# A weave planner's TensorE prices and three buffers are changed in a four-layer convolution kernel

## The chip, the cores and the metric

The kernel runs as one program on one core of a Trainium2 chip. A core has five engines that work side by side, each through its own instructions in the order in which they were written: TensorE (matrix products, PE in the profile, with its weight loads as PEld), VectorE (DVE), ScalarE (ACT), GpSimd (POOL) and SyncE (SP), which here only issues DMA transfers. An engine waits for another by a semaphore. The metric is the device time of one execution in microseconds; three executions of the kernel before took 6713.72, 6719.5 and 6728.77, a median of 6719.5.

## The reference

The input x has 16 images of 32 channels of 128 x 128. Four layers follow one another, each of the form x = x + layer(groupnorm(x)):

```python
x = x + _L0_conv_ref(_gn(x), W2, b2, W1, b1)        # a recurrence over 128 skewed columns
x = x + _L1_conv_ref(_gn(x), weight)                # -sum |patch - w|, quantised, 3 x 3, 32 -> 32
x = x + _L2_conv_ref(_gn(x), weights1)              # Hartley transform, 32 x 32 modes mixed, back
x = x + _L3_conv_ref(_gn(x), conv1_w, ..., deconv3_b)  # edge filters, then a small U-shaped net
```

Layer 1 is the bulk: for each of 32 outputs, 32 inputs, 9 taps and every pixel, an absolute difference is added up. Layer 3 makes five filtered and normalised copies of its input, and then conv1 (160 to 32 channels, 3 x 3), three poolings and small convolutions (conv2 to conv4), three doublings of size, each followed by a convolution (conv5 to conv7), and multiplies the result with its input.

## The kernel before, in words

Channels lie on the 128 partitions, four images at a time: four groups of four images. The time falls into three parts.

**Layer 0** (function `stage0`) is a recurrence that needs everything else to wait. The change does not touch it.

**Layer 1 with later layers woven in.** Class `Differences` makes, for each half image (32 of them, two to an image, which the code calls a batch), 72 *maps*: relu(q - w) of 128 x 8192 numbers, made either by DVE (L760) or by ACT (L757). TensorE adds each map to four accumulators with 16 matmuls (`sums`, L647), and adds a linear term in 9 steps (`linear`, L662). A map lies in one of three tiles for DVE and two for ACT, so its maker can't go on when TensorE is more than that behind. Layers 2 and 3 of a group (class `After`) need all four images of that group from layer 1, and nothing else; so group 0's are put between the maps of group 1, and so on. What is not placed when the last map is made is left to the tail.

**The tail** (`drain`) writes out what is left of group 2's layers 2 and 3, and all of group 3's, taking a step of one and a step of the other by a planned time.

What decides the order is a planner that runs while the program is written, class `Weave`. It keeps planned clocks for TensorE, DVE and ACT. `After.work` is a generator: each of its parts issues instructions and then yields. A positive number is the planned TensorE time of what was issued; a negative one is a wait in planned time; SUMMED waits until the planned sums are done; ("done", v) until a put-off piece is done; ("after", n) until batch n is finished. After each map, `Weave.advance` is given the time at which TensorE is next needed for a map's sum, and places steps as long as they fit:

```python
start = max(self.pe, self.ready)
if start + 1.0 > due + SLACK:
    return
us = self.step()
```

A map's sum costs PE_US of planned TensorE time (L708), a linear step what L669 says, and what is then left of the interval is filled by `keep_busy` (L671), up to four times four matmuls with a weight of zeros, which add nothing to the result and keep TensorE running. Pieces for DVE, ACT and SP are put off with `weave.later(us, ...)` and written when the planned time has come. The engines know nothing of the plan: `keep_order` fixes the order on each engine, and semaphores do the rest. So a plan that is wrong makes an engine wait, and never makes a wrong result.

The later layers of one group, with the lines at which they yield, are in order: `forward` (a transform of rows and columns, L1119, L1134, L1091), `mixing` (32 steps of 16 matmuls, L1206, whose weights of 1 MB a piece lie in a pool of "t_w" tiles), `back` (L1270, then L1315 with the residual from HBM), `statistics` (products of rows of the normalised image, L1420, to learn the five filters' means and deviations), the folding of those into conv1's weights (L1553, tables v loaded by POOL), the sums for the cut edges (L1713), `conv1` (8 chunks of 16 rows, each 25 taps of 16 matmuls, L1739, with its edges at L1756, pooled at L1666), conv2 to conv4 (`small_layers`, L1589), and the doublings with their convolutions (`round`, L905), the last of them in `last`, which multiplies with the input and stores (L1868, L1838).

`frames` holds a ring of tiles of 20 padded rows each, which `back` fills first, `statistics` normalises and refills (by `load` for chunks not seen, then by `again` for the first chunks of conv1), and `conv1` reads. How many tiles each pool has while the weave runs is in `buffers` (L966); in the tail group 3 has a larger set of its own (L513), which stays. GpSimd issues its table loads (L1408, L1492, L1538) [...]; all other DMAs but a few at the start are SP's.

## Time and profile before

| | us |
|---|---|
| median of three runs | 6719.5 |
| profiled execution | 6728.15 |
| its span, first to last instruction | 6726.4 |
| TensorE busy (its matmuls) | 5379.0 |
| DVE busy | 5537.9 |
| ACT busy | 5464.8 |
| POOL busy | 63.0 |
| first map starts | 685.0 |
| last map starts, on ACT | 5595.0 |
| mean granted TensorE clock | 0.919 |

Busy times are unions of an engine's instructions; a matmul's end is modelled, and matmuls in different parts of the array overlap, so a busy TensorE is not one at its peak. Lines such as L647 are lines of the kernel before. "A <- B" in a row of the profile is "written from", in a list of waits "waited for". The 40 slices of the page are 168 us each. Times in a window count from the first instruction.

### The profile page before, as it was taken

What the parts mean: (1) busy time and instruction counts of PE and PEld (TensorE: products, weight loads), DVE (VectorE), ACT (ScalarE), POOL (GpSimd) and SP (SyncE); (2) the same over time, 40 slices, a digit from 0 to 9 for tenths busy, and PEclk for the clock granted to TensorE, in tenths of its full rate; (3) what the DMA queues carried; (4) which work ended last, traced back from release to release, by engine and by line L of the source; (5) the groups of instructions that cost most, each with busy time, mean ns of one, the idle gap of its engine ahead of it and who ended that gap; (6) DMA issues with size and microseconds to landing.
All of it is one profiled execution on the core that took longest, in us unless ns stands there. A gap on an engine that the chain in (4) does not pass through costs nothing.

```text
span 6726.4 us, 271378 instructions
## 1 busy us (share of the span) xinstructions
PE 5379.0 (80%) x127212; PEld 2798.3 (42%) x127212; DVE 5537.9 (82%) x6839; ACT 5464.8 (81%) x3210; POOL 63.0 (1%) x67
## 2 busy tenths in 40 slices
PE   3798777788777879997877878998787785886896
PEld 3675333333343433333333433333334442453574
DVE  7898999999999889998999989999899995144122
ACT  3998999999999989999999999999899993121112
POOL 0000000000000000000000000000000000000000
PEclk9999899999989989998999889999899897997897
DMA  7553312212253632213453552221354353355314
GB/s 318 204 190 123 81 49 64 61 31 66 71 140 113 178 94 60 62 38 72 101 147 93 174 149 68 66 63 42 87 128 138 103 155 119 125 188 141 83 39 107
DMA packets 380776, 728.20 MB, mean 108 GB/s; under 512 B 73284, under 2 KB 225348, under 8 KB 368772
## 3 DMA queue, kind: packets, MB, share of 16 engines
q1 hardware_dynamic: 372180, 676.41, 35.2%
q0 software_dynamic: 7040, 33.80, 1.5%
q8 instruction: 995, 16.30, 1.0%
q14 instruction: 129, 1.06, 0.1%
q10 hardware_dynamic: 432, 0.64, 0.0%
HBM read 510.69 MB, written 200.00 MB: 106 GB/s over the span
## 4 chain that ended last, share of the span: by engine, by line
issue 33%; PE 29%; DVE 20%; ACT 14%; DMA 3%; SPq 1%; POOL 0%; DVEq 0%; ACTq 0%; POOLq 0%
DVE d_dve L760 12%; PE acc L1739 11%; ACT d_act L757 9%; PE acc L647 8%; PE acc L905 3%; PE pg L223 3%; ACT gt L237 2%; DMA v<-fold_d 1%; PE acc L1589 1%; PE acc L1420 1%; ACT junk L198 1%; DVE y L1677 1%; DVE stat L124 1%; DMA x_in<-in_x_dram 1%; ACT th L247 1%
## 5 line engine op out<-in xcount | busy, mean ns | idle before, releaser
L757 ACT ACTIVATE d_act<-q,neg 128x8192 f16<-128x8192 f16 (+1 forms) x629 | 4450.5, 7154 | 102.7 <-PE acc L647 81.1
L760 DVE TENSOR_SCALAR d_dve<-q,qw 128x8192 f16<-128x8192 f16 (+1 forms) x1675 | 3864.3, 2360 | 214.5 <-PE acc L647 195.6
L647 PE MATMUL acc<-d_dve,sel 128*32 128x512 f16 x26800 | 1879.4, 404 | 436.3 <-DVE d_dve L760 344.6
L647 PEld LDWEIGHTS <-sel 128*32 128x32 f16 x36864 | 1021.0, 101 | 2124.4 <-issue 1475.8
L1739 PE MATMUL acc<-xp,wf 32*32 32x512 f32 x25600 | 1001.7, 611 | 32.6 <-issue 27.2
L647 PE MATMUL acc<-d_act,sel 128*32 128x512 f16 x10064 | 740.0, 416 | 345.2 <-ACT d_act L757 333.4
L1680 ACT ACTIVATE y<-pooled,b 32x128 f32<-32x128 f32 x472 | 188.7, 400 | 552.6 <-DVE pooled L1666 546.3
L1739 PEld LDWEIGHTS acc<-xp,wf 32*32 32x32 f32 x25600 | 417.6, 104 | 377.6 <-issue 295.8
L677 PE MATMUL acc<-q,zero 128*32 128x512 f16 x6720 | 484.2, 400 | 0.0
L905 PE MATMUL acc<-y,u_conv 32*32 32x256 f32 (+1 forms) x9728 | 358.7, 461 | 85.1 <-issue 68.7
L223 PE MATMUL pg<-h,wb 64*64 64x20 f32 (+15 forms) x8192 | 342.0, 306 | 58.0 <-DVE h L251 32.9
L237 ACT ACTIVATE gt<-pg,bias 128x20 f32<-128x20 f32 (+15 forms) x1024 | 332.7, 385 | 39.3 <-PE pg L223 37.1
L223 PEld LDWEIGHTS pg<-h,wb 64*64 64x64 f32 x8192 | 252.1, 151 | 133.5 <-DVE h L251 80.9
L677 PEld LDWEIGHTS <-zero 128*32 128x32 f16 x6720 | 200.6, 101 | 187.3 <-issue 42.7
L1868 DVE SCALAR_TENSOR_TENSOR xr<-acc,l_one,xr 128x512 f32<-128x512 f32 x128 | 87.2, 744 | 229.8 <-PE acc L905 179.7
L1420 PE MATMUL acc<-xp 32*64 32x204 f32 (+3 forms) x8576 | 240.8, 339 | 40.6 <-issue 40.5
L905 PEld LDWEIGHTS acc<-y,u_conv 32*32 32x32 f32 x9728 | 162.0, 109 | 216.9 <-issue 168.1
L1420 PEld LDWEIGHTS acc<-xp 32*64 32x64 f32 (+1 forms) x8576 | 169.1, 132 | 124.4 <-issue 118.9
L1838 ACT ACTIVATE xr<-xr,l_ms 128x1024 f32<-128x1024 f32 x64 | 68.7, 1146 | 182.1 <-DVE xr L1868 171.9
L223 PE MATMUL pg<-xn,wb 64*64 64x2 f32 (+63 forms) x4096 | 183.5, 290 | 25.6 <-issue 17.0
L1774 DVE TENSOR_TENSOR acc<-acc,cut 128x4 f32<-128x4 f32 x256 | 35.2, 164 | 200.6 <-PE acc L1739 198.3
L1589 PE MATMUL acc<-y,w_conv 32*32 32x512 f32 (+2 forms) x4608 | 153.6, 487 | 37.1 <-issue 28.9
(218 smaller groups left out, 3624.5 us busy)
## 6 DMA issues: line engine op xcount, KB each, us to landing
q<-q_d SPq DMA_DIRECT2D x128, 536.2 KB, 10.3
xp<-xn_d SPq DMA_DIRECT2D x64, 660.0 KB, 5.1
xp<-x_d SPq DMA_DIRECT2D x56, 640.0 KB, 5.3
xr<-xn_d SPq DMA_DIRECT2D x64, 528.0 KB, 11.3
x_in<-in_x_dram SPq DMA_DIRECT2D x16, 2048.0 KB, 14.7
xn<-in_xs_dram SPq DMA_DIRECT2D x64, 512.0 KB, 7.1
res<-in_x_dram SPq DMA_DIRECT2D x64, 512.0 KB, 8.6
x_d<-res SPq DMA_DIRECT2D x64, 512.0 KB, 4.8
```

The source lines that it names most:

```text
L223: nc.tensor.matmul(bank[c][q][64 * pair : 64 * pair + 64, :, :width], wb[half, 4 * kind + KIND[q]].rearrange("p b o -> p (b o)"), v[half], ...
L237: nc.scalar.activation(gt[:, q, :, :n], bank[c][q][:, :, :n], AF.Tanh if q == G else AF.Sigmoid, bias=bias[:, KIND[q] : KIND[q] + 1],)
L647: self.nc.tensor.matmul(acc[k][32 * j : 32 * j + 32, :], self.sel16[:, i // 9, :], d[:, row : row + 4, c : c + W], start=first, stop=last,)
L677: self.nc.tensor.matmul(acc[k][32 * j : 32 * j + 32, :], self.zero, q[:, :4, :W], start=False, stop=False)
L757: nc.scalar.activation(dst, src, AF.Relu, bias=self.neg[:, i : i + 1])
L760: nc.vector.tensor_scalar(dst, src, self.qw[:, i : i + 1], 0.0, ALU.subtract, ALU.max)
L905: nc.tensor.matmul(acc[blk][32 * j : 32 * j + 32, o : o + rows * n], t[part, 4 * par + tap, :], src[part, top : top + rows, left : left + ...
L1420: nc.tensor.matmul(gram[blk][j : j + width, at : at + n], xp[part, l, 2 + j : 2 + j + width], xp[part, rows, j : j + width + 4], start=sta ...
L1589: nc.tensor.matmul(acc[blk][32 * j : 32 * j + 32, : rows * n], wc[name][part, tap, :], src[part, at : at + rows, kw : kw + n], start=tap == 0,
L1680: nc.scalar.activation(d, s, AF.Identity, bias=bj)
L1739: nc.tensor.matmul(acc[blk][32 * j : 32 * j + 32, :], tap_of("all", tap)[rows], xp[rows, 4 * j + kh : 4 * j + kh + 4, kw : kw + W], start= ...
L1868: nc.vector.scalar_tensor_tensor(v, acc[blk].rearrange("p (b r w) -> p r w b", b=2, w=64), one[:, blk : blk + 1], v, ALU.add, ALU.mult,)
```

## The change

It has three parts. The first sets new planned TensorE times for most steps; no instruction's work changes by it, only where in the order the planner puts it, and how many matmuls by zeros it adds. A map's sum goes from 1.0 to 0.88, a linear step from 0.45 to 0.36, four matmuls by zeros from 0.25 to 0.22; among the later layers a mixing step goes from 1.0 to 0.3 (with five written waits that go from 2.5 to 5.5), a step of `back` from 1.1 to 0.35 and from 0.8 to 0.4, a row of `statistics` from 0.5 to 0.38, the cut sums from 0.6 to 0.35, a tap of conv1 from 1.15 to 1.06 and its edges from 0.3 to 0.1, and the convolutions after it get a new formula, which for 512 columns gives 1.06 in place of 1.15 and for 256 columns 0.67 in place of 0.65 (conv3) or 1.05 (`round`). The second gives the pool of mixing weights a fourth tile and the ring of frames a third while the weave runs. As 8 chunks are no multiple of 3 tiles, conv1 counts on where `statistics` stopped, with `window`, which takes chunk ch from the tile of chunk ch + 8. The third sets the memory for GpSimd's descriptors to 4,096 bytes of each partition, where it had the default.

```diff
--- before.py
+++ after.py
@@ -484,7 +484,7 @@
 
 
 
-DVE_US, ACT_US, PE_US = 2.36, 7.15, 1.0
+DVE_US, ACT_US, PE_US = 2.36, 7.15, 0.88
 LATE = 1.5
 SLACK, CLOCK = 3.0, 1.0
 SUMMED = ("summed",)
@@ -666,18 +666,18 @@
                     start=False,
                     stop=False,
                 )
-        self.weave.pe = max(self.weave.pe, self.weave.now) + 0.45
+        self.weave.pe = max(self.weave.pe, self.weave.now) + 0.36
 
     def keep_busy(self, acc, q, until):
 
 
         start = max(self.weave.pe, self.weave.now)
-        for k in range(min(int((until - start - 0.1) / 0.25), 4)):
+        for k in range(min(int((until - start - 0.1) / 0.22), 4)):
             for j in range(4):
                 self.nc.tensor.matmul(
                     acc[k][32 * j : 32 * j + 32, :], self.zero, q[:, :4, :W], start=False, stop=False
                 )
-            self.weave.pe = start + 0.25 * (k + 1)
+            self.weave.pe = start + 0.22 * (k + 1)
 
     def run(self, tc, ctx, weave):
         nc, R, P = self.nc, self.R, self.P
@@ -910,7 +910,7 @@
                         stop=tap == 3,
                         skip_group_check=True,
                     )
-            yield rows * n / 512 * 0.2 + 0.95
+            yield rows * n / 512 * 0.78 + 0.28
             if tap != 2:
                 continue
             for j in range(4):
@@ -963,7 +963,7 @@
         self.nc, self.tc, self.side, self.ps, self.cst, self.bias = nc, tc, side, ps, cst, bias
         self.a, self.d, self.stat, self.out = a, d, stat, out
         self.spare, self.banks = None, 0
-        self.buffers = {"t_x": 4, "xm": 3, "xw": 2, "t_w": 3, "t_r": 4, "frames": 2, "gm": 3, "e_v": 3, "l_x": 2}
+        self.buffers = {"t_x": 4, "xm": 3, "xw": 2, "t_w": 4, "t_r": 4, "frames": 3, "gm": 3, "e_v": 3, "l_x": 2}
         store = [d["up"][i] for i in range(3)]
         self.up5 = Composed(nc, sm, a, "deconv1", "conv5", bias[:, 7:8], bias[:, 4:5], store[0])
         self.up6 = Composed(nc, sm, a, "deconv2", "conv6", bias[:, 8:9], bias[:, 5:6], store[1])
@@ -1106,7 +1106,7 @@
                         steps[n] = weave.later(2.0, store)
 
                     steps[n] = outs[n] = weave.summed(out)
-                    return 1.45
+                    return 1.2
 
                 yield -4.0
                 t1s, ta, ready = {}, {}, {}
@@ -1124,7 +1124,7 @@
                         weave.dve += 0.7
 
                     ready[n, 0] = weave.summed(out)
-                    return 1.05
+                    return 0.9
 
                 def turned(n):
 
@@ -1133,7 +1133,7 @@
                     for a in range(4):
                         nc.tensor.transpose(p[:, 128 * a : 128 * a + 128], ta[n][:, a, :], cst["ident128"])
                     ready[n, 1] = weave.summed(lambda: scaled(n, p))
-                    return 1.5
+                    return 1.0
 
                 for n in range(10):
                     if n < 8:
@@ -1212,9 +1212,9 @@
                 )
             if ky % 4 == 3 and len(wt) < M1 // 4:
                 wt.append(self.weights(wp, len(wt)))
-            yield 1.0
+            yield 0.3
             if ky % 4 == 3 and 8 < ky < M1 - 1 and not weave.draining:
-                yield -2.5
+                yield -5.5
         yield SUMMED
         zs = wp.tile([128, 2, 4, 4, 32], F32, name="zs", bufs=1)
         for half in range(2):
@@ -1274,7 +1274,7 @@
                                 start=True,
                                 stop=True,
                             )
-                    yield 1.1
+                    yield 0.35
                 yield SUMMED
                 for blk in range(4):
                     dst = o1[:, :, blk, 16 * oh : 16 * oh + 16].rearrange("p h o -> p o h")
@@ -1319,7 +1319,7 @@
                             start=True,
                             stop=True,
                         )
-                yield 0.8
+                yield 0.4
                 if previous:
                     yield -3.2
                     take_out(*previous)
@@ -1347,6 +1347,7 @@
             nc.vector.memset(t[:, :, W + 3], 0.0)
 
         chunk = lambda ch: ring[ch % len(ring)]
+        window = lambda ch: ring[(ch + 8) % len(ring)]
 
         def parts(ch, half):
 
@@ -1386,9 +1387,9 @@
         def again(ch, half):
 
             own = slice(10 * half, 10 * half + 10)
-            nc.sync.dma_start(chunk(ch)[:, own, :], padded(ch, own.start, own.stop))
-
-        return load, normalise, store, again, chunk
+            nc.sync.dma_start(window(ch)[:, own, :], padded(ch, own.start, own.stop))
+
+        return load, normalise, store, again, chunk, window
 
     def statistics(self, g, pool, frames, sides, out, tables):
 
@@ -1399,7 +1400,7 @@
 
 
         nc, cst, weave = self.nc, self.cst, self.weave
-        load, normalise, store, again, chunk = frames
+        load, normalise, store, again, chunk, _ = frames
         ahead = self.buffers["frames"]
         ready = {(n // 2, n % 2): normalise(n // 2, n % 2, 0.5 + 4.0 * n) for n in range(2 * ahead)}
         tables_ahead = self.buffers["gm"]
@@ -1441,7 +1442,7 @@
                 first, last = len(own), min(H - r, 3)
                 if first < last:
                     products(xp, l, slice(l + first, l + last), 64, 68 * first, False, r == H - 3)
-                yield 0.5
+                yield 0.38
                 if l not in (9, 17):
                     continue
 
@@ -1593,7 +1594,7 @@
                                 start=tap == 0,
                                 stop=tap == 8,
                             )
-                    yield rows * n / 512 * 1.0 + 0.15
+                    yield rows * n / 512 * 0.78 + 0.28
                 yield SUMMED
                 for blk in range(4):
                     evict(r, rows, acc[blk][:, : rows * n], blk)
@@ -1690,7 +1691,7 @@
             size = PARTS[n][4] * PARTS[n][5]
             return wf[:, const if i == size else at + i, :]
 
-        _, _, _, again, chunk = frames
+        _, _, _, again, _, window = frames
         ahead = self.buffers["frames"]
         p = self.acc()
         for j in range(4):
@@ -1718,7 +1719,7 @@
                             stop=tap == 10,
                             skip_group_check=True,
                         )
-                yield 0.6
+                yield 0.35
         yield SUMMED
         cut = pool.tile([128, 4, 2, 8, 4], F32, name="cut")
         for blk in range(4):
@@ -1727,7 +1728,7 @@
 
         spreads = []
         for ch in range(H // R):
-            xp = chunk(ch)
+            xp = window(ch)
 
             acc = [self.acc() for _ in range(4)]
             edge = {0: ("t", 0, 0, 1), H // R - 1: ("b", 3, 3 * W, 17)}.get(ch)
@@ -1761,8 +1762,8 @@
                                     stop=False,
                                     skip_group_check=True,
                                 )
-                            yield 0.3
-                yield 1.15
+                            yield 0.1
+                yield 1.06
             yield SUMMED
             if ch + ahead < H // R:
                 for half in range(2):
@@ -2031,7 +2032,7 @@
     from concourse.bass_utils import run_bass_kernel_spmd
 
     arrays, at = layout(inputs)
-    nc = bacc.Bacc("TRN2", target_bir_lowering=False, num_devices=1)
+    nc = bacc.Bacc("TRN2", target_bir_lowering=False, num_devices=1, dynamic_dma_scratch_size=4096)
     arrays = {f"in_{n}_dram": t for n, t in arrays.items()}
     a = {}
     for n, t in arrays.items():
```

## The prediction

> **What bounds the kernel now.** I read the 40 slices first, then the costliest groups, then busy time by stretch, then the waits of the long stretch, and last the order of time on TensorE.

> ```profile
> PE   3798777788777879997877878998787785886896
> DVE  7898999999999889998999989999899995144122
> ACT  3998999999999989999999999999899993121112
> PEclk9999899999989989998999889999899897997897
> ```

> Three parts show: a recurrence (slices 1 to 4), a long part in which DVE and ACT are full (to slice 33), and a tail in which they are nearly idle and only TensorE works.

> ```profile
> L757 ACT ACTIVATE d_act<-q,neg 128x8192 f16<-128x8192 f16 (+1 forms) x629 | 4450.5, 7154 | 102.7 <-PE acc L647 81.1
> L760 DVE TENSOR_SCALAR d_dve<-q,qw 128x8192 f16<-128x8192 f16 (+1 forms) x1675 | 3864.3, 2360 | 214.5 <-PE acc L647 195.6
> ```

> These are the 2,304 difference maps. DVE makes one in 2.36 us and ACT one in 7.15 us, so together 1/2.36 + 1/7.15 = 0.424 + 0.140 = 0.564 maps a us. Columns of the next view: stretch, its length, then busy time by engine.

> ```profile
> core 0: us, PE busy (x) PEld busy (x) DVE busy (x) ACT busy (x) POOL busy (x), PEclk, DMA share, GB/s
> 685.00:1838.00 1153.00, 900.62 (x15886) 432.22 (x15889) 1134.19 (x878) 1129.12 (x176) 0.00 (x0) 0.94 0.23 57
> 1838.00:5603.00 3765.00, 3142.30 (x70725) 1437.22 (x70721) 3508.20 (x3000) 3631.26 (x990) 48.93 (x38) 0.92 0.38 103
> 5603.00:6726.00 1123.00, 870.06 (x28302) 552.41 (x28294) 333.47 (x911) 190.46 (x372) 11.67 (x22) 0.87 0.41 117
> 4074.00:4614.00 540.00, 520.19 (x11624) 198.17 (x11615) 507.60 (x326) 527.20 (x188) 0.00 (x0) 0.98 0.21 53
> 5605.00:5647.00 42.00, 3.80 (x205) 3.37 (x205) 26.51 (x68) 3.81 (x2) 3.73 (x7) 0.50 1.02 319
> ```

> Row 2 is the stretch with both jobs: maps, and the later layers woven in. Its work, in time at the full map rate, is (3508.2 x 0.424 + 3631.3 x 0.140) / 0.564 = 3,539 us; 226 us (6.0%) are idle. Row 3 is the tail: what the weave had not placed. By the first and last records of each line, group 0's later layers run from 1838 to 3385, group 1's from 3434 to 4981, each 1,547 us for 1,200 us of maps; group 2's start at 5029 and have reached only the end of the statistics at 5603. The tail does its conv1 (5668 to 6018) and the rest to 6414 in between group 3's steps, and then group 3's alone. So the end is set by how much the weave places before 5603.

> ```profile
> PE acc L647 <- ACT d_act L757: 231.9, 140, 5.3
> PE acc L647 <- DVE d_dve L760: 221.2, 172, 6.6
> DVE d_dve L760 <- PE acc L647: 187.9, 107, 8.5
> ACT d_act L757 <- PE acc L647: 60.5, 28, 7.3
> ```

> In that stretch (us in total, times, longest) TensorE waits for maps as much as the map makers wait for TensorE: it has room, not a lot.

> ```profile
> 2644.60 1.14 PE L1739 MATMUL acc<-xp,wf 32*32 32x512 f32 x32
> 2645.67 1.06 PE L647 MATMUL acc<-d_dve,sel 128*32 128x512 f16 x16
> 2646.66 1.15 PE L1739 MATMUL acc<-xp,wf 32*32 32x512 f32 x32
> 2647.74 1.05 PE L647 MATMUL acc<-d_dve,sel 128*32 128x512 f16 x16
> 2648.72 1.15 PE L1739 MATMUL acc<-xp,wf 32*32 32x512 f32 x32
> ```

> From start to start, a conv1 tap takes 1.07 us and a map's sum 0.98, together 2.05. The plan has 1.15 + 1.0 = 2.15 for the pair; after the change, 1.06 + 0.88 = 1.94. So the plan goes from 5% too slow to 5% too fast, switches between the two counted.

> [...] Sums that follow one another start 0.877 us apart in the trace: 0.88 is a full-clock price. [...] No run yet shows the small ring.

> **The change, part by part.**

> *Ring and buffers.* [...] Were it too small, the seven v tables that follow the first three in each group would come late, each by its landing time of 7.3 us at most: 51 us, on the path only in the last group. I take 0 and keep +51 as the far end. The third frame makes the first burst six loads of 640 KB where four are now, on SP ahead of q's loads (5.3 us each, q waits cost DVE 15.7 us in the whole run): 0 to +10 us a group, cover is the 64 maps between two q loads; I take 0. The fourth mixing tile moves one 1 MB load (6.1 us) ahead. Bytes in all stay. What the frame buys: a frame's normalising is due 20 us after the load's issue; with two frames it is needed 1.5 chunks later, which at 18 us a chunk was 27 us and at the new 12 would be 18, late; with three it is 2.5 x 12 = 30.

> *Pace.* Maps come every 2.18 us here (144 x 12 maps in 3,765). The plan keeps for a map 1.0 + (9 x 0.45 + 2.6)/72 = 1.09 us of TensorE, leaving half, so a planned us of later work lasts 2.0 us. After, 0.88 + (9 x 0.36 + 2.6)/72 = 0.96, and it lasts 1.77. Check on what is measured: statistics 128 x 0.5 x 2 + 16 of waits = 144 (measured 144); first half of back 32 x 1.1 x 2 = 70 (70); decoder and last layers 88 x 2 + 70 of waits = 246 (246). Hence by stage of group 1, us before and after: forward 61, 44 (24.8 x 1.77); mixing 63, 45 (9.6 x 1.77 + 27.5 of waits, five of them longer); back's first half 70, 25 (11.2 x 1.77 + 5); second half 104, 99 (held by its 3.2 us waits); statistics 144, 102 (48.6 x 1.77 + 16); cut sums 31, 21; conv2 to conv4 94, 86; decoder and last 246, 191 (61.7 x 1.77 + 70 gives 179; two tiles for x hold some of it). Conv1, 540 before: the plan says 216 x 1.77 + 40 = 423, but TensorE needs for 219 sums and 200 taps 209 x 2.05, 27 linear steps at 0.6 and 9 for edges, 454; with 4% lost I take 470. The other 194 us are waits that stay. Sum 1,277, with the 48 us between groups 1,325 a group. Four batches take 1,318 (3,954/3, below), so the wait for the next group's maps does not bind.

> *The long part.* Group 2's later half moves in. By the rows of its lines, a quarter each: DVE 114 us (L1666 28, L1774 9, L1677 37, L1868 22, L1553 and small ones 18), ACT 80 (L1680 63, L1838 17): (114 x 0.424 + 80 x 0.140)/0.564 = 106 us. Idle: before, 27 us in this conv1 stage (row 4: DVE idle 32, ACT 13), 31 in group 0's, and the other 168 over 2,681 us, so 63 in a group's other 1,003. After, 40 in each of three conv1 stages, since TensorE sets their pace, and 63 elsewhere: 309. So 3,539 + 106 + 309 = 3,954 in place of 3,765. Before 1838 more dummy matmuls fill the planned gaps (0.22 each): +5. The long part ends at 5603 + 189 + 5 = 5797. Group 2 would end at 1843 + 3 x 1325 = 5818: 21 us left.

> *The tail*, then almost group 3 alone, from its end backwards: last 183 kept; conv1 293 becomes 200 x 1.04 (the undisturbed pitch after 6437) + 14 = 222, as group 2's matmuls are gone; fold and cut sums 84 to 75; statistics 125 to 100; norms and frames 46 to 40; back's second half 94 to 54 (DVE 16 x 2.7); first half 57 to 27; mixing and its stores 109 to 64 (8 MB at the 319 GB/s of row 5 is 26); forward ends 77 sooner, held by the eight input loads that run until 5645. Saved: 71 + 9 + 25 + 6 + 40 + 30 + 45 + 77 = 303, so 820; with the 21 us left and what they hold up, 855.

> *Sum.* 5797 + 855 = 6652, against 6726.4: -74 us. The profiled run lasted 1.8 us longer than its span, and 8.7 us longer than the median shown (it lies at the top of the three): 6645.

> **Rivals.** *TensorE becomes the bound and it ends slower (0.24).* The plan promises 5% more than a switching TensorE gives, the clock outside conv1 is 0.80 to 0.95, and dummies fill the gaps in which it could catch up. DVE and ACT then idle over a sum. It decides at L = 3645/(1 - x) with 1843 + L + 840 = 6726: x = 9.8% idle in the long stretch; at 11%, 4,096 us and some 6770. Against it: outside conv1 the later layers have more wait than work. *Stalls do not grow (0.15):* idle stays 226 us, as the waits above show TensorE waiting as often; 83 us less, and some of it back in the tail as group 2 has less time: about 6570. *The weave hardly moves (0.13):* conv1 is 96% busy on TensorE now; if bursts keep a group at 1,480 us, group 2 starts 133 us sooner, the long part grows 47 and the tail falls 70: about 6695. That the ring or a frame does nothing is no case of its own: at 0 both are inside these.

> **How the numbers follow.** Likeliest 0.48, 6645, its own range 6595 to 6695. No change means within 0.2%, 13 us, about what a measurement of this kernel can tell. Faster: 0.46 + 0.15 + 0.08; same 0.06; slower 0.25. The range leaves one in ten below the third case's lower half and one in ten in the upper part of the slower case: 6545 to 6765.

> **What would show it.** The last map at about 5797 (5603 now), idle of some 8%; group 1's later layers about 1,280 us long (1,547), conv1 about 470; group 2's conv1 before the last map; group 3's conv1 in one piece of about 222 us; no wait of wf for v beyond today's. It is wrong if the long part grows past 280 us, if TensorE's delays to L760 and L757 double (248 us now), or if the tail stays over 950.

## The result, and the profile after

The changed kernel takes 6793.73 us (median of 4 runs, 6787.79 to 6795.69); the kernel before took 6718.79 beside it. The ratio is 1.0108, with a 95% interval of 1.0091 to 1.0126: slower by 1.1%, where 1.1% faster was forecast. The measured time lies above the whole stated range, 6545 to 6765.

From the page of the profiled execution, some of its slices, one line of its DMA queues and the two costliest groups (a slice is 170 us here):

```profile
PE   3797788888877799978877799888777999865696
...
DVE  7897999999988888888987888889887898873222
ACT  3998999999989789989987899889887899850012
...
q8 instruction: 1020, 16.71, 1.0%
...
L757 ACT ACTIVATE d_act<-q,neg 128x8192 f16<-128x8192 f16 (+1 forms) x628 | 4455.2, 7149 | 361.0 <-PE acc L647 337.4
L760 DVE TENSOR_SCALAR d_dve<-q,qw 128x8192 f16<-128x8192 f16 (+1 forms) x1676 | 3876.3, 2360 | 464.2 <-PE acc L647 443.6
```

The tail is shorter by two slices, more than forecast. But the 9s of DVE and ACT have become 8s and 7s: the maps cost what they did (2,360 and 7,149 ns), and their makers now wait for TensorE's sums 443.6 and 337.4 us, where it was 195.6 and 81.1. By stretch (the same columns as before; the third row is the pause before group 1's later layers, the last three are parts of them):

```profile
core 0: us, PE busy (x) PEld busy (x) DVE busy (x) ACT busy (x) POOL busy (x), PEclk, DMA share, GB/s
...
1833.00:6040.00 4207.00, 3571.72 (x84582) 1678.94 (x84578) 3643.19 (x3300) 3718.69 (x1149) 45.47 (x45) 0.92 0.37 100
6040.00:6794.00 754.00, 498.02 (x16487) 392.22 (x16476) 227.75 (x642) 101.76 (x188) 7.96 (x15) 0.78 0.43 129
3133.00:3252.00 119.00, 103.35 (x1722) 48.05 (x1718) 117.23 (x87) 118.15 (x21) 0.00 (x0) 0.94 0.36 92
3397.00:3442.00 45.00, 29.18 (x1175) 16.28 (x1170) 26.74 (x15) 29.05 (x5) 0.00 (x0) 0.70 0.19 39
3592.00:3711.00 119.00, 98.34 (x2836) 58.27 (x2824) 80.99 (x72) 87.37 (x49) 0.00 (x0) 0.91 0.64 193
3803.00:4262.00 459.00, 453.50 (x10531) 179.27 (x10523) 400.67 (x266) 419.09 (x169) 0.00 (x0) 0.99 0.17 46
```

The long part lasts 4,207 us (3,765 before) and holds 3,661 us of work at the full map rate, counted as in the prediction; 546 us are idle (226). The tail is 754 us (1,123). The fourth, fifth and sixth rows are where the idle is: in the first half of `back` DVE is busy 26.7 of 45 us, in `statistics` 81 of 119, in conv1 401 of 459. The third row is the opposite: from 3133 to 3252 DVE and ACT are full, and nothing is woven in, because group 0's later layers are done and group 1's have to wait for the fourth of their images. Three such pauses, 119, 126 and 71 us, make 316 us in which TensorE had room and no later work; before the change the two between groups took 49 and 48 us.

The waits of the long part (us in total, times, longest):

```profile
DVE d_dve L760 <- PE acc L647: 439.2, 248, 16.0
...
ACT d_act L757 <- PE acc L647: 318.7, 127, 17.9
```

They were 187.9 and 60.5, the longest 8.5 and 7.3. A wait of 16 us is no slip of one sum: something holds TensorE for long. Its own order of time shows what (first half of `back`, group 1):

```profile
3396.58 1.22 PE L1270 MATMUL acc<-cw,zi 32*32 32x32 f32 x121
3406.02 1.29 PE L1270 MATMUL acc<-cw,zi 32*32 32x32 f32 x103 [8.22 <-issue]
3407.24 1.90 PE L647 MATMUL acc<-d_dve,sel 128*32 128x512 f16 x16
3409.07 1.95 PE L1270 MATMUL acc<-cw,zi 32*32 32x32 f32 x137
3412.96 0.39 PE L1270 MATMUL acc<-cw,zi 32*32 32x32 f32 x23 [1.94 <-issue]
```

121 matmuls go in 1.22 us, and then TensorE stands for 8.22 us, waiting for nothing that the profile shows. The line q8 of the page is the clue: 1,020 transfers of 16,384 bytes, labelled instruction. TensorE has 130,384 matmuls and as many weight loads, and 260,768 / 1,020 is 256 to a transfer (before, 254,424 / 995, 256 too): by these counts I read it as TensorE's program being fetched. In the records of the DMA engines, one of these starts at 3391.80 and the next at 3403.20, then 3407.10, 3410.60 and 3414.09. The same stretch in two parts, and third the same half of `back` in the kernel before:

```profile
3394.00:3404.00 10.00, 3.80 (x173) 2.31 (x161) 7.85 (x4) 10.00 (x3) 0.00 (x0) 0.90 1.00 214
3405.00:3442.00 37.00, 28.38 (x1086) 15.59 (x1087) 21.89 (x12) 21.05 (x4) 0.00 (x0) 0.67 0.02 4
3620.00:3682.00 62.00, 49.53 (x1572) 25.56 (x1564) 61.80 (x30) 62.00 (x10) 0.00 (x0) 0.93 0.01 3
```

In the first, the DMA engines are full (share 1.00) with data, and no fetch starts until 3403.20. In the second they are nearly empty (0.02), and fetches still start no closer than 3.37 us. In the third, at the old prices, DVE and ACT are busy throughout. Over the whole run the closest two fetches are 3.25 us apart, one in ten closer than 3.54. 256 instructions per 3.5 us are 73 a us. A step of `back`'s first half has 32 matmul records and 32 loads: at 73 a us that is an estimated 0.88 us, where the old price was 1.1 and the new one 0.35, the pace of a short burst (121 in 1.22 us above, so 32 in 0.32).

### The profile page after: what moved, and what is told of

Its sections match the earlier page's. It is cut to its first block, busy times and chain, and to the rows that moved or that the text cites. A ratio compares the mean times of both kernels' runs of the same rounds, so it can differ in the third digit from the quotient of the medians.

```text
span 6793.9 us, 277725 instructions
## 1 busy us (share of the span) xinstructions
PE 5483.8 (81%) x130384; PEld 2906.3 (43%) x130384; DVE 5566.2 (82%) x6870; ACT 5463.9 (80%) x3185; POOL 55.8 (1%) x67
## 3 DMA queue, kind: packets, MB, share of 16 engines
q8 instruction: 1020, 16.71, 1.0%
q14 instruction: 128, 1.05, 0.0%
## 4 chain that ended last, share of the span: by engine, by line
PE 41%; issue 25%; DVE 21%; ACT 7%; DMA 4%; SPq 1%; POOL 0%; DVEq 0%; ACTq 0%; POOLq 0%
PE acc L647 14%; PE acc L1740 13%; DVE d_dve L760 11%; ACT d_act L757 4%; PE acc L905 4%; PE pg L223 3%; PE acc L1590 2%; ACT gt L237 2%; DVE y L1678 1%; PE acc L1421 1%; DVE stat L124 1%; PE acc L677 1%; ACT junk L198 1%; DMA xp<-x_d 1%; DMA v<-fold_d 1%
## 5 line engine op out<-in xcount | busy, mean ns | idle before, releaser
L757 ACT ACTIVATE d_act<-q,neg 128x8192 f16<-128x8192 f16 (+1 forms) x628 | 4455.2, 7149 | 361.0 <-PE acc L647 337.4
L760 DVE TENSOR_SCALAR d_dve<-q,qw 128x8192 f16<-128x8192 f16 (+1 forms) x1676 | 3876.3, 2360 | 464.2 <-PE acc L647 443.6
L647 PE MATMUL acc<-d_dve,sel 128*32 128x512 f16 x26816 | 1863.2, 400 | 472.2 <-DVE d_dve L760 381.7
L647 PEld LDWEIGHTS <-sel 128*32 128x32 f16 x36864 | 996.2, 99 | 1979.1 <-issue 1288.7
L1740 PE MATMUL acc<-xp,wf 32*32 32x512 f32 x25600 | 950.0, 603 | 20.3 <-issue 18.5
L647 PE MATMUL acc<-d_act,sel 128*32 128x512 f16 x10048 | 721.8, 407 | 142.5 <-ACT d_act L757 120.4
L677 PE MATMUL acc<-q,zero 128*32 128x512 f16 x9892 | 683.3, 391 | 0.7 <-issue 0.7
L677 PEld LDWEIGHTS <-zero 128*32 128x32 f16 x9892 | 294.9, 99 | 263.2 <-issue 37.7
L905 PE MATMUL acc<-y,u_conv 32*32 32x256 f32 (+1 forms) x9728 | 312.3, 462 | 79.3 <-issue 67.9
L1366 ACT ACTIVATE xp<-xp,shift,stats 128x1280 f32<-128x1280 f32 (+1 forms) x64 | 91.6, 1433 | 303.0 <-DVE shift L1333 186.1
L1421 PEld LDWEIGHTS acc<-xp 32*64 32x64 f32 (+1 forms) x8576 | 185.0, 140 | 143.7 <-issue 113.7
```

The lines of the kernel that those rows point to most:

```text
L647: self.nc.tensor.matmul(acc[k][32 * j : 32 * j + 32, :], self.sel16[:, i // 9, :], d[:, row : row + 4, c : c + W], start=first, stop=last,)
L677: self.nc.tensor.matmul(acc[k][32 * j : 32 * j + 32, :], self.zero, q[:, :4, :W], start=False, stop=False)
L757: nc.scalar.activation(dst, src, AF.Relu, bias=self.neg[:, i : i + 1])
L760: nc.vector.tensor_scalar(dst, src, self.qw[:, i : i + 1], 0.0, ALU.subtract, ALU.max)
L905: nc.tensor.matmul(acc[blk][32 * j : 32 * j + 32, o : o + rows * n], t[part, 4 * par + tap, :], src[part, top : top + rows, left : left + ...
L1366: nc.scalar.activation(v, v, AF.Identity, bias=self.shift3, scale=self.stats3[:, 1])
```

## The experiments

Each ratio is to the kernel before, run beside it, which took 6719 us beside the changed kernel and 6733 to 6737 beside the others; the expectations count from 6719. Idle is worked out as in the prediction, DVE's and ACT's idle time weighted by their map rates, and comes from one profiled execution of each kernel. "Conv1" and "elsewhere" are the idle of group 0 and group 1 in conv1 and in the rest of their later layers.

| run | ratio to before | a group, us | idle conv1 | idle elsewhere | idle, long part | last map | tail |
|---|---|---|---|---|---|---|---|
| before | | 1547, 1547 | 31, 28 | 70, 72 | 226 | 5602 | 1124 |
| changed | 1.0108 | 1300, 1307 | 58, 54 | 121, 138 | 546 | 6040 | 754 |
| buffers | 0.9974 | 1552, 1535 | 37, 25 | 68, 64 | 216 | 5594 | 1131 |
| prices | 1.0107 | 1297, 1295 | 64, 50 | 112, 130 | 548 | 6048 | 760 |
| sum_price | 1.0011 | 1381, 1334 | 37, 50 | 126, 87 | 455 | 5947 | 783 |
| map_side_new | 0.9882 | 1436, 1454 | 51, 47 | 59, 67 | 278 | 5688 | 975 |
| supply | 0.9926 | 1408, 1403 | 44, 56 | 66, 67 | 331 | 5761 | 916 |
| supply_95 | 0.9925 | 1450, 1472 | 47, 58 | 60, 65 | 301 | 5713 | 973 |
| dense_cheap | 0.9977 | 1410, 1416 | 29, 40 | 106, 103 | 364 | 5788 | 923 |
| light_only | 0.9969 | 1411, 1412 | 52, 62 | 75, 70 | 371 | 5806 | 923 |
| tap_dear | 0.9875 | 1483, 1437 | 31, 20 | 59, 58 | 208 | 5613 | 1027 |
| sum_cheaper | 0.9944 | 1395, 1436 | 54, 52 | 79, 71 | 346 | 5775 | 909 |

**Buffers or prices.** `buffers` is the kernel before with the third frame, the fourth mixing tile and the small ring (`dynamic_dma_scratch_size=4096`); `prices` is the changed kernel without them:

```diff
-        self.buffers = {..., "t_w": 4, "t_r": 4, "frames": 3, ...}
+        self.buffers = {..., "t_w": 3, "t_r": 4, "frames": 2, ...}
...
-    nc = bacc.Bacc(..., dynamic_dma_scratch_size=4096)
+    nc = bacc.Bacc(...)
```

> The kernel before with the third frame, the fourth mixing tile and the 4,096 byte ring, all prices as before. If the prices cost the time (my theory): within 0.3% of the kernel before, about 6719, statistics still near 144 us. If the buffers or the ring do (rival): most of the 75 us, about 6790, with wf waiting longer for v or q coming late.

> The changed kernel with two frames, three mixing tiles and the default ring: the new prices alone. If the prices cost the time: about 6795, as changed. If the buffers do: about 6720. A third possibility: two frames are too few at the new pace, and statistics, 119 us in the changed kernel, gets longer; then over 6810.

Measured: 0.9974 (0.9967 to 0.9981) and 1.0107 (1.0092 to 1.0122). All of the loss is the prices'. The buffers alone gain a little: idle in `statistics` falls from 14 and 18 us to 6 and 7. At the new pace they make no difference that shows (`statistics` idles 28 and 31 us without them, 33 and 37 with them). The ring costs nothing that shows: wf waits 24.6 us for v in `buffers` and 23.1 in the kernel before, 8.4 in the changed kernel and 9.4 in `prices`, which has the default ring.

**The sum's price or the later layers'.** `sum_price` puts PE_US back to 1.0 in the changed kernel. `map_side_new` is the changed kernel with every later layer's price as before, so that only the sum, the linear step and the zeros are new:

```diff
-DVE_US, ACT_US, PE_US = 2.36, 7.15, 0.88
+DVE_US, ACT_US, PE_US = 2.36, 7.15, 1.0
```

> The changed kernel with the price of a map's sum back at 1.0 and nothing else. If promising a sum at full clock is what starves the map makers: idle in a group's later layers falls from 180 us to about 100, a group takes some 1,300 us with no gap before the next, the last map at about 5740, time about 6520 to 6600. If the later layers' own prices are too low (rival): the idle stays over 150 us a group and the time over 6750.

> The changed kernel with all prices of the later layers back at the old ones; only the sum at 0.88, the linear step at 0.36 and the zeros at 0.22 are new. If the sum's price starves the makers: idle near 150 us a group, a group about 1,450 us, time 6700 to 6760. If the later layers' prices do: idle near 100 us a group, and with a group about 1,450 us some 6650 to 6700.

My theory, that a sum priced at full clock (0.88; sums that follow one another in the kernel before start 0.86 to 0.88 us apart, at a granted clock of 1.00) is what starves the makers, fell as it stood: with a sum at 1.0 the idle elsewhere is still 126 and 87 us, and with the low sum and the old later layers it is 59 and 67, less than before, and the kernel is faster: 0.9882 (0.9865 to 0.9898). But the sum's price is part of the loss. Put back alone, it takes the time to 1.0011 (1.0004 to 1.0019) of before; the 6744 us lie between the two expectations, and the pauses before groups 1 and 2 shrink from 119 and 126 us to 53 and 54. The later layers' new prices cost some 0.4% beside a sum at 1.0 (`buffers` to `sum_price`) and 2.3% beside one at 0.88 (`map_side_new` to the changed kernel); the low sum gains 0.9% beside the old later layers and costs 1.0% beside the new ones. So the loss of 1.1% is that of both together. (The linear step and the zeros stay new in `sum_price`, so the first comparison is not quite of one thing.) Why the two don't simply add is not shown. More matmuls by zeros are not the cause alone: L677 has 6,720 records before and 9,892 in the changed kernel, but also 8,180 in `map_side_new`.

**Which of the later layers' prices.** After the fetches had been seen, I sorted the steps by the number of TensorE's instructions. `supply` is the changed kernel with no step priced below one us for 73 instructions; `supply_95` adds a sum at 0.95:

```diff
-        self.weave.pe = max(self.weave.pe, self.weave.now) + 0.36
+        self.weave.pe = max(self.weave.pe, self.weave.now) + 0.44
...
-            yield rows * n / 512 * 0.78 + 0.28
+            yield max(rows * n / 512 * 0.78 + 0.28, 0.88)
...
-                    yield 0.35
+                    yield 0.9
...
-                yield 0.38
+                yield 0.46
...
-                yield 0.35
+                yield 0.88
```

(In this order: linear, rounds and small convolutions alike, first half of `back`, `statistics`, cut sums; the short correction matmuls of a round go from 0.4 to 1.1, the second half of `back` from 0.4 to 0.44, conv1's edges from 0.1 to 0.22, and mixing has its old price and waits.)

> The changed kernel, where no step is priced below 1 us for 73 of TensorE's instructions (the fastest its instruction fetches, 256 each, come one after another): back's first half 0.9, cut sums 0.88, statistics 0.46, rounds and small convolutions at least 0.88, linear 0.44, edges 0.22, mixing as before. If dense steps of small matmuls wait for their instructions (my theory now): idle in those stages falls to about what the kernel before has, 90 to 115 us a group, a group about 1,410 us, time about 6640. If the low price of a sum is to blame: idle stays near 150 a group, time over 6720.

> As the last, and a sum at 0.95, nearer to the 0.98 seen between other steps. If conv1's remaining idle of some 50 us comes from the sum's price: 35 there, a group about 1,445 us, time 6620 to 6650. If the sum's price doesn't matter: a longer group and nothing gained, 6650 to 6680.

`supply`: 0.9926 (0.9911 to 0.994). The idle elsewhere is 66 and 67 us, from 121 and 138. The first half of `back` of group 1 in `supply`, in the columns of the stretches above, shows it:

```profile
3456.00:3518.50 62.50, 46.67 (x1604) 23.50 (x1600) 56.05 (x31) 59.60 (x11) 0.00 (x0) 0.89 0.35 77
```

It takes 62.5 us in place of 45, and DVE is busy 56 of them; idle fell from 18 us to 6, in group 0 from 13 to none, and in the cut sums from 9 and 14 to 1 and none. (They idled 10 us a group in the kernel before already: the old 0.6 is under the estimated 0.88 too.) In `statistics` it fell from 33 and 37 only to 21 and 18. The time is not the 6640 expected but 6683: idle is 110 and 123 us a group where 90 to 115 were expected, and conv1 keeps 44 and 56 of it. `supply_95` (0.9925, 0.9906 to 0.9944) has 47 and 58 there, where 35 was expected: a sum at 0.95 in place of 0.88 does not take conv1's idle away.

`dense_cheap` and `light_only` are complements. The first is the kernel before, with the new buffers and new prices in the dense steps only (`back`, cut sums, `statistics`, rounds, mixing); the second has all the other new prices and not these:

```diff
-            yield 1.0
+            yield 0.3
             if ky % 4 == 3 and 8 < ky < M1 - 1 and not weave.draining:
-                yield -2.5
+                yield -5.5
...
-                yield 0.5
+                yield 0.38
```

> The kernel before with the new buffers, and only the dense steps at the new prices (back, cut sums, statistics, rounds, mixing); sum 1.0, conv1 1.15, forward and small convolutions as before. If those steps wait for their instructions: idle rises from 97 to about 150 us a group there, a group about 1,420 us, and the time is 6690 to 6740 although the weave is faster. If a low price of a step does no harm while the sum keeps 1.0: idle near 100 us, time about 6640.

> The complement of dense_cheap: the changed kernel with the dense steps (back, cut sums, statistics, rounds, mixing) at the old prices, and all other prices and buffers as changed. If the harm lies in the dense steps' prices: idle 105 to 120 us a group, of it about 50 in conv1, a group about 1,410 us, time 6640 to 6670. If it lies in the other prices: idle over 150, time over 6720.

Both have groups of 1,410 us. `dense_cheap` idles 106 and 103 us elsewhere and gains next to nothing (0.9977, 0.9969 to 0.9986) although its groups are 135 us shorter than before. `light_only` idles 75 and 70 there, but 52 and 62 in conv1, and gains little more (0.9969, 0.996 to 0.9978; 6710, where 6640 to 6670 was expected, with idle of 127 and 133 us a group where 105 to 120 was; its profiled run was its slowest). So the idle elsewhere goes with the dense steps' prices in every kernel of the table: 87 to 138 us in the four that have them low, 58 to 79 in the eight that don't. But the other prices cost as well, in conv1.

**Is it the instructions?** `narrow`, which ran once, is the changed kernel with a quarter of the columns in 23 of conv1's 25 taps, as many instructions as before. Conv1's sums are incomplete in it.

```diff
-                            acc[blk][32 * j : 32 * j + 32, :],
+                            acc[blk][32 * j : 32 * j + 32, : 512 if tap in (0, 24) else 128],
...
-                            xp[rows, 4 * j + kh : 4 * j + kh + 4, kw : kw + W],
+                            xp[rows, 4 * j + kh : 4 * j + kh + (4 if tap in (0, 24) else 1), kw : kw + W],
```

> The changed kernel with 23 of conv1's 25 taps at 128 columns in place of 512, as many instructions as before; conv1's sums are therefore incomplete, and group 3's conv1 in the tail, alone on TensorE, is what is read (216 us now). If instructions set its pace (64 a tap): still 165 us or more. If the array does: about 70 us.

Group 3's conv1 in the tail, alone on TensorE, from the busy time of line 1740 in that stretch (columns: length, matmuls busy, weight loads busy, clock, DMA share, GB/s); first the changed kernel, then `narrow`:

```profile
6392.00:6608.00 216.00, 208.34 (x6400) 169.36 (x6400) 0.99 0.09 29
```

```profile
6278.50:6487.00 208.50, 131.65 (x6400) 94.84 (x6400) 0.79 0.09 30
```

With some 70% of the columns gone, 216 us become 208 (the clock fell from 0.99 to 0.79, far too little to make up for it). So 13,472 instructions, with the edges, took 208 us, or 65 a us, even with a quarter of the columns in 23 of 25 taps. TensorE's order of time in `narrow` shows what it waits for:

```profile
6440.74 1.91 PE L1740 MATMUL acc<-xp,wf 32*32 32x128 f32 x128 [1.23 <-issue]
6444.48 1.90 PE L1740 MATMUL acc<-xp,wf 32*32 32x128 f32 x128 [1.84 <-issue]
6447.95 1.90 PE L1740 MATMUL acc<-xp,wf 32*32 32x128 f32 x128 [1.57 <-issue]
6451.97 1.90 PE L1740 MATMUL acc<-xp,wf 32*32 32x128 f32 x128 [2.12 <-issue]
```

A row is four taps, 128 matmuls with 128 loads: the 256 instructions of one transfer. They go in 1.9 us, 135 a us, so TensorE's own pace with them is not the limit, and then it stands. In this conv1 it stands 50 times for over 0.5 us, 40 of them exactly 256 instructions after the last, and 49 of the 50 end 2.1 to 3.0 us after a fetch began. So in this conv1 of `narrow` the fetches set the pace. With all its columns, in the changed kernel, the same conv1 hardly waits: TensorE's loads wait 11 us for "issue" and not 96, the taps start evenly, some 1.04 us apart, and the fetches mostly some 4 us apart. So it runs near the limit that `narrow` shows, but what sets its own pace is not shown. In the weave, where a tap and a sum have 96 instructions in 2.05 us (47 a us), the columns do count: conv1's idle there fell from 58 and 54 us to 15 and 17 with narrow taps, while `narrow` still idles 125 and 134 us elsewhere.

The same sign can be looked for in the long part. TensorE's waits of over 2 us that end 2.1 to 3.0 us after a fetch began come to 129 us before (37 of them) and 227 us in the changed kernel (65); all its other waits of that length to 322 and 294. Some may end there by chance, but only the waits of this kind grew. How much of the 320 us that DVE and ACT idle more comes from them, and how much from other delays, is not measured.

**Conv1.** `tap_dear` is `map_side_new` with a tap at 1.25 in place of 1.15, `sum_cheaper` the same with a sum at 0.80 in place of 0.88.

```diff
-                yield 1.15
+                yield 1.25
```

> As map_side_new (old prices for the later layers, new for the maps' side), with a tap of conv1 at 1.25 in place of 1.15. If conv1's idle comes from the price of tap and sum together (2.03 in map_side_new, 2.13 then, 2.05 measured, 2.15 in the kernel before): idle in conv1 falls from 50 to about 30 us, conv1 takes about 535 us, and the time is 6650 to 6680, since what the maps win the tail loses. If it doesn't: conv1 still idles 45 us or more.

> As map_side_new with the sum at 0.80 in place of 0.88, under what any row shows. If a low price of the sum does harm of its own: idle over 150 us a group and the time over 6720. If only the pair price in conv1 and the dense steps matter: idle in conv1 some 70 us, elsewhere as in map_side_new, a group about 1,390 us, time 6650 to 6700.

`tap_dear`, in the columns of the stretches above, its long part and group 1's conv1:

```profile
1839.00:5613.00 3774.00, 3214.72 (x73876) 1476.50 (x73872) 3545.59 (x3070) 3626.31 (x1019) 56.84 (x45) 0.93 0.39 106
3977.50:4483.00 505.50, 491.18 (x11256) 185.73 (x11248) 480.76 (x314) 498.11 (x184) 0.00 (x0) 1.00 0.21 54
```

Idle in conv1 is 31 and 20 us, from 51 and 47. It goes with what the plan asks for a tap and a sum together, against the 2.05 us that the pair takes: at 2.13 and 2.15 conv1 idles 20 to 40 us, at 1.94 to 2.06 it idles 37 to 64, with no clear order within that range. `tap_dear` is the fastest of all kernels here, 6647.61 us, 0.9875 of before (0.9858 to 0.9892), though not clear of `map_side_new`. `sum_cheaper` (0.9944, 0.9929 to 0.9959) idles no more in conv1 than `map_side_new`, 54 and 52 where some 70 was expected, and far from 150 a group. But it is 0.6% slower than `map_side_new`, and its long part idles 346 us where that one's idles 278: a sum below what any row shows does some harm of its own.

## Why the prediction was wrong

*Pace: right.* A group was to take 1,277 us and took 1,300, 1,307 and 1,284; conv1 was to take 470 and took 469, 459 and 460. The dense stages came out longer than forecast (statistics 117 to 120 for 102, `back`'s first half 37 to 46 for 25), rounds near it (183 to 198 for 191).

*Work moved in: right.* 106 us were forecast, 122 came.

*Idle: wrong, and this is the step that failed.* "40 in each of three conv1 stages ... and 63 elsewhere: 309". Conv1 idled 58, 54 and 54, and the rest 121, 138 and 116 a group: 541, and 5 in the pauses. The 63 was carried over from the kernel before as if a stage's stalls kept their length when its steps are priced lower; it was not worked out from the pace at which TensorE's instructions come in those stages (some 73 a us, by the fetches above), and the rival was set aside because "outside conv1 the later layers have more wait than work". The lists of waits named "issue" before TensorE's instructions, and I did not ask what was being waited for. The old prices of the dense steps, 1.1 for `back`, 0.5 for `statistics`, 1.05 for a round, cover the estimated 0.88, 0.46 and 0.88 us that their instructions take at 73 a us; the new ones, 0.35, 0.38 and 0.67, don't. That these low prices make the idle is shown by `dense_cheap`, `light_only` and `supply`; that fetches are what TensorE waits for is shown in `narrow` and for some of the waits of the changed kernel. The low price of a sum had to come with them for the loss.

*The pauses: wrong.* "The wait for the next group's maps does not bind": with the maps slowed, four batches took about 1,400 us and not 1,318, and the weave stood for 119 and 126 us before groups 1 and 2. With the maps at that pace, a group of 1,300 us could not have begun the next any sooner than one of 1,350, by the usual 48 us between groups.

*The tail: shorter than forecast.* 855 were forecast and 754 came. Group 2 was done 71 us before the last map, so the 35 us kept for it fell away; and `back`'s second half, norms and frames, and fold with cut sums took 35, 19 and 51 us where 54, 40 and 75 were forecast. Group 3's conv1 in one piece took 216 for 222.

*The sum closes:* from 6652, +237 of idle, +16 of work, -10 before the first group, -101 in the tail is 6794, the span.

*The rival* that ends slower named the place: DVE and ACT idling over a sum, decided at 9.8% idle. It came at 13.0%. Its reasons, switches and a low clock (0.64 to 0.97 by stage of group 1 outside conv1 before, 0.70 to 0.93 after), are not what the runs point to outside conv1; there it is the dense steps. In conv1 it is the pair's price against 2.05, which the prediction had set out, as far as one run, `tap_dear`, shows. Of the signs that the prediction gave of being wrong, two came: the long part grew by 442 us, and TensorE's delays to L760 and L757 went from 248 to 758 us in it. *Buffers:* I took 0, and they gain 0.3% alone. *The ring* at 0 was right, as far as wf's waits for v show it (23.1 us before, 8.4 after); why 4,096 bytes are enough no run shows, and the 51 us for a ring too small was my estimate. *Readings:* in the long part before, TensorE waited 453 us for maps and the makers 248 us for TensorE, so it was not as much but more; four images of maps took 1,255 us there (3,765/3), not 1,200; and the factor 1.77 is 1.79 by its own working. The last two move the sum by little.

## What to carry to other kernels

A step's cost to a planner is not its fastest pitch in a trace: don't price it under the time it takes between other steps (here a tap and a sum took 2.05 us, and conv1 idled 51 and 47 us with the pair planned at 2.03, 31 and 20 at 2.13), or under its instruction count at the rate at which instructions came (here 73 a us), above all where many small matmuls follow one another. Test prices together: here a low sum gained 0.9% beside the old prices of the later layers and cost 1.0% beside the new ones. In an order that is fixed beforehand, prices that are too low can take more from the engines that set the pace than the earlier finish gives back, and one somewhat too high can cost little: 1.25 for a tap measured at 1.07 is in the fastest kernel here. Before work is made to end sooner, look at what it waits for next: here the following group could not start.
